# Attention block on one core: the last head's division by 128x8 columns, and the first image through two DMA queues

## The chip, the cores and the metric

The kernel runs on one core of one Trainium2 chip. A core has a matrix engine (TensorE, PE in the profile; its weight loads are listed apart as PEld), a vector engine (DVE), a scalar engine (ACT), GpSimd (POOL) and a sync engine (SP) that here only issues DMAs. The metric is the device time of one execution in microseconds; the time of a kernel is the median of several runs.

## What is computed

The block is a group norm, multi-head self-attention over the 1024 pixels of each image, a projection and a residual, all in float32. There are 16 images of 512 channels, 4 heads of 128 channels and 8 groups. Cut to what matters:

```python
b, c, h, w = x.shape                      # 16, 512, 32, 32
xn = group_norm(x, 8) * gamma + beta
qkv = einsum('oc,bchw->bohw', qkv_w, xn) + qkv_b
q, k, v = heads(split(qkv, 3))            # 4 heads of 128
attn = softmax(einsum('bhnd,bhmd->bhnm', q, k) * 128 ** -0.5)
out = einsum('bhnm,bhmd->bhnd', attn, v)
out = einsum('oc,bchw->bohw', proj_w, out) + proj_b
return x + out
```

## The kernel before

**Steps.** The fast path runs 16 images x 4 heads x 8 blocks of 128 keys, 512 steps in all. A step makes scores of 128 keys against 1024 queries in two halves of 512 (L607), takes the exponential on ACT without subtracting a maximum (L612), adds it to a running sum `tot` on DVE (L620), and multiplies `v` by it into `po` (L675), which ACT copies to `os_` (L682). The projections (q and k, v, output) are done with Strassen's seven products, two levels deep for most of them; the sums that they need are DVE subtractions and additions, and their pieces are spread over the steps by a written plan (`plan_head`).

**Order.** The program is traced in Python order, and a planner that simulates the engines then orders each engine's instructions: it takes what is ready by its own model of time, earlier-traced work first. Each engine runs its list strictly in that order. Tiles come from pools; tiles with one tag share that tag's buffers, and a tile waits until its buffer is free. The PSUM tag "s" of pool `ps_s` has two buffers. DMAs issued by SP and ACT use eight completion semaphores in turn, so a DMA waits until the one eight before it in the planner's order has landed.

**Division.** After a head's eight steps the softmax denominators are needed: the sum of `tot` over its 128 partitions. For all heads but the last, `denominators` (L622) makes them in a small 32x32 form, takes the reciprocal there, and broadcasts it to 128 partitions through DRAM into `rinv`; `divide` multiplies `os_` by it. The last head of the last image uses `last_division` (L648): a product with a 128x128 matrix of ones puts the denominators of 512 queries on all partitions at once; DVE takes the reciprocal of that 128x512 tile and multiplies `os_` by it, for each half. `last_span` (L660) takes the reciprocal of the reciprocal on 32 partitions to recover `l`, and keeps the sum over the queries of max(l, 1/l) in the last column of `spans`. At the end all of `spans` is summed (`total`, `most`) and compared with a limit; if it is over, the whole block is computed again on a general path.

**The last projection** (`last_projection`, L748) follows the last step with one level of Strassen. `x_` and `y_` are two PSUM banks each (`lx`, `ly`), `z_` (`lz`) takes tag "s". Products 1 and 5 do not read the last head's output; product 2 reads it in its second chunk, and so does product 6, whose operand `t2` is a DVE subtraction (L253, `sums_of_b`). `copy` keeps `x_` on ACT before the next product accumulates into it. `add` (L764) adds a product to the residual tile `y`, and its last call for a tile issues the output DMA.

**The start.** `load_x(0)` issues the first image as eight transfers of 256 KB on SP (L199). DVE takes statistics of each (`bn_stats` L40, `bn_aggr` L41), then a short chain of small operations on PE, DVE and POOL gives scale and shift, and DVE and ACT normalise. Behind the image, SP loads weights of v (`wv`, L373) and of q and k (`st`, L287); ACT loads five small vectors (L215: `gamma_sb` and so on) and its function table (L206).

Of the kernel before, what the change touches and what calls it, by code (L numbers as in the profile page):

```python
# [10 lines left out]
F32 = mybir.dt.float32  # L11
I32 = mybir.dt.int32
AF = mybir.ActivationFunctionType
ALU = mybir.AluOpType
AX = mybir.AxisListType

P = 128
HEADS = 4
GROUPS = 8
EPS = 1e-5  # L20
BLK = 32
HALF = 512
# [65 lines left out]
def attention_block(  # L88
# [35 lines left out]
    with ExitStack() as fast:  # L124
        fast_path(fast, tc, x, sources, out, consts, flag, dims)
# [28 lines left out]
def fast_path(ctx, tc, x, sources, out, consts, flag, dims):  # L154
# [5 lines left out]
    nc = tc.nc  # L160
    B, C, N, NCC, NH2, NB, GC, SCALE = dims
# [6 lines left out]
    one = ctx.enter_context(tc.tile_pool(name="one", bufs=1))  # L168
# [8 lines left out]
    lpool = ctx.enter_context(tc.tile_pool(name="l", bufs=1))  # L177
    upool = ctx.enter_context(tc.tile_pool(name="u", bufs=2))
    ypool = ctx.enter_context(tc.tile_pool(name="y", bufs=4))
    gn = ctx.enter_context(tc.tile_pool(name="gn", bufs=2))  # L180
    dpool = ctx.enter_context(tc.tile_pool(name="rows", bufs=4, space=DRAM))
    kept = ctx.enter_context(tc.tile_pool(name="kept", bufs=1, space=DRAM))
    ps_s = ctx.enter_context(tc.tile_pool(name="ps_s", bufs=2, space=PSUM))
# [1 line left out]
    ps_a = ctx.enter_context(tc.tile_pool(name="ps_a", bufs=2, space=PSUM))  # L185


    spans = one.tile([BLK, B * HEADS], F32, name="spans")
    ones = one.tile([BLK, 1], F32, name="ones")
    ones_sq = one.tile([P, P], F32, name="ones_sq")  # L190
    xs, xb, vs, qs, ks, os_, ob = {}, {}, {}, {}, {}, {}, {}
    mvs, scaled = {}, {}

    def load_x(b):
        for c in range(NCC):
            xs[b, c] = xpool.tile([P, N], F32, tag="x", name=f"x_{b}_{c}")
            for half in range(NH2 if b == 0 else 1):
                i = ts(half, HALF) if b == 0 else ds(0, N)
                nc.sync.dma_start(xs[b, c][:, i], x[b, ts(c, P), i])  # L199


    load_x(0)
# [46 lines left out]
    def sums_of_b(b, rows=(1, 2), chunks=range(KC)):  # L249

        def sub(o, i, j):
            for k in chunks:
                nc.vector.tensor_sub(b[o][k], b[i][k], b[j][k])  # L253

        if 1 in rows:
            sub("t1", "b12", "b11")
        if 2 in rows:
            sub("t2", "b22", "t1")
            sub("t3", "t2", "b11")
            sub("t4", "b21", "t2")  # L260
# [336 lines left out]
    ps, tot, po, rinv, last_eviction = {}, {}, {}, {}, {}  # L597
    steps = B * HEADS * NB

    def where(s):  # L600
        bh, j = divmod(s, NB)
        return (*divmod(bh, HEADS), j)
# [44 lines left out]

    def last_division(b, h):  # L648

        t = tot.pop((b, h))  # L650
        for half in range(NH2):
            l = ps_s.tile([P, HALF], F32, tag="s", name=f"l_{half}")
            nc.tensor.matmul(l, ones_sq, t[:, ts(half, HALF)], start=True, stop=True)
            i = ts(half, HALF)
            r = lpool.tile([P, N], F32, tag="rinv", name=f"rinv_{b}_{h}") if half == 0 else r
            nc.vector.reciprocal(r[:, i], l)
            nc.vector.tensor_mul(os_[b, h][:, i], os_[b, h][:, i], r[:, i])
        return r

    def last_span(r):  # L660

        l = lpool.tile([P, N // BLK, BLK], F32, tag="tt", name="l_last")
        l = l.rearrange("p c m -> p (c m)")[:BLK, :]
        nc.vector.reciprocal(l, r[:BLK, :])
        nc.vector.scalar_tensor_tensor(
            l, l, 1.0, r[:BLK, :], ALU.mult, ALU.max,
            accum_out=spans[:, B * HEADS - 1 : B * HEADS],
        )

    def weighted_sum(s, half):  # L670
        b, h, j = where(s)
# [47 lines left out]
    late = {}  # L719

    def last_loads(what):


        if what == "x":
            late["y"] = []
            for c in range(NCC):
                t = xpool.tile([P, N], F32, tag="x", name=f"y_{c}")
                nc.sync.dma_start(t, x[B - 1, ts(c, P), :])
                late["y"].append(t)
            return  # L730
        late["w"] = []
        for g in range(4):
            t = qkpool.tile([P, N], F32, tag=f"qk{g % 2}", name=f"wl_{g}")
            t = t.rearrange("p (i m) -> p i m", m=HALF)
            first = 2 * g
            n = slice(1, 2) if g == 0 else slice(0, 2)
            nc.sync.dma_start(t[:, n], store["last"][:, first + n.start : first + 2])
            late["w"] += [t[:, 0], t[:, 1]]
# [9 lines left out]
    def last_projection(b):  # L748


        y, bl = late["y"], ob[b]
        x_, y_, z_, kept_ = {}, {}, {}, {}

        def mm(acc, r, p, first):
            for k in range(KC):
                nc.tensor.matmul(  # L756
                    acc, late["w"][p][:, ds((r * KC + k) * P, P)], bl[FACTORS[p][1]][k],
                    start=(first and k == 0), stop=(k == KC - 1), skip_group_check=True,
                )

        def add(row, r, half, a, done):
            o = 2 * row + r
            t = y[o][:, ts(half, HALF)]
            nc.vector.tensor_add(t, t, a)  # L764
            if done:
                (nc.sync, nc.scalar)[r].dma_start(out[b, ts(o, P), ts(half, HALF)], t)

        def copy(r, n):
            t = upool.tile([P, HALF], F32, tag=n, bufs=1 if n == "u3" else 2, name=f"l_{n}_{r}")
            nc.scalar.copy(t, x_[r])  # L770
            kept_[n, r] = t

        for r in range(2):
            x_[r] = ps_a.tile([P, HALF], F32, tag="x", name=f"lx_{r}")
            mm(x_[r], r, 1, True)
            copy(r, "p1")
        recip = last_division(b, HEADS - 1)
        sums_of_b(bl, (2,), (1,))
        for r in range(2):
            y_[r] = ps_a.tile([P, HALF], F32, tag="y", name=f"ly_{r}")  # L780
            mm(y_[r], r, 5, True)
            add(0, r, 0, kept_["p1", r], False)
        for r in range(2):
            z_[r] = ps_s.tile([P, HALF], F32, tag="s", name=f"lz_{r}")
            mm(z_[r], r, 2, True)
            add(0, r, 0, z_[r], True)
        for r in range(2):
            mm(x_[r], r, 6, False)
            copy(r, "u2")
        last_span(recip)  # L790
        for r in range(2):
            add(0, r, 1, kept_["u2", r], False)

        total = gn.tile([BLK, 1], F32, tag="total", name="total")
        nc.vector.tensor_reduce(total, spans, AX.X, ALU.add)
        for r in range(2):
            mm(x_[r], r, 7, False)
            copy(r, "u3")
            add(1, r, 1, kept_["u3", r], False)
            add(1, r, 1, y_[r], True)  # L800
        most = ps_s.tile([P, HALF], F32, tag="s", name="most")
        nc.tensor.matmul(most[:1, :1], total, ones, start=True, stop=True)
        ok = gn.tile([1, 1], F32, tag="fine", name="fine")
        nc.vector.tensor_scalar(ok, most[:1, :1], LIMIT, None, ALU.is_le)
        fine.append(ok)
        for r in range(2):
            mm(x_[r], r, 4, False)
            add(1, r, 0, x_[r], True)
        for r in range(2):
            mm(y_[r], r, 3, False)  # L810
            add(0, r, 1, y_[r], True)

    def plan_head(b, h):
# [7 lines left out]
        elif h == 1:  # L821
# [6 lines left out]
            if b + 1 == B:  # L828
                plan[0].append(lambda: last_loads("x"))
            else:  # L830
                plan[0].append(lambda: load_x(b + 1))
                spread(plan, [lambda c=c: stats_chunk(b + 1, c) for c in range(NCC)], 2, 6)
                plan[5].append(lambda: stats_group(b + 1))
                plan[6] += [
                    lambda c=c, half=half: normalise(b + 1, c, half)
                    for half in range(NH2) for c in range(NCC)
                ]
        elif b + 1 == B:
            if h == 2:
                plan[0].append(lambda: last_loads("w"))  # L840
                plan[2].append(last_bias)
            else:
                os_[b, h] = opool.tile([P, N], F32, tag="o", name=f"o_{b}_{h}")
                plan[3].append(lambda: o_blocks(b))
                plan[3].append(lambda: sums_of_b(ob[b], (1,)))
                plan[4].append(lambda: sums_of_b(ob[b], (2,), (0,)))
        elif b + 1 < B:
            if h == 2:
                plan[0].append(lambda: x_sums(b + 1))
                spread(plan, staggered([v_units(b + 1, jj) for jj in range(2)]), 1, NB)  # L850
            else:
                spread(plan, staggered(qk_groups(b + 1, 0)), 0, NB)
# [34 lines left out]
    for s in range(steps + 1):  # L887
        units = []
        if s < steps:
            b, h, j = where(s)  # L890
# [5 lines left out]
        for half in range(NH2):  # L896
# [6 lines left out]
            n = (len(units) + 1) // 2  # L903
            run(units[half * n : (half + 1) * n])
        if s > 0:
            del ps[s - 1]

    last_projection(B - 1)
    nc.vector.tensor_scalar(flag, fine[0], -1.0, 1.0, ALU.mult, ALU.add)

# [130 lines left out]
```

## Time and profile before

| what | value |
|---|---|
| median of 4 runs | 3237.96 us (3236.84 to 3238.95) |
| the profiled execution | 3237.0 us, span 3235.1 us, granted clock 0.999 |
| DVE busy 3200 to 3205, 3205 to 3210, 3210 to 3215.4 | 4.98, 5.00, 5.40 us |
| `rinv<-l` 128x512 reciprocal (L656) | 2 x 3320 ns |
| `l_last<-rinv` 32x1024 reciprocal (L664) | 1 x 6532 ns |
| `l_last` 32x1024 max and sum (L665) | 1 x 1206 ns |
| `l<-tot,ones_sq` (L653) | 4 PE instructions, 592 ns each |
| `o<-o,rinv` 128x512 (L657) | 2 x 650 ns |
| x transfers (L199) | 8 x 256 KB, 4.0 us median from issue to landing |
| DMA traffic | 357.32 MB, mean 110 GB/s over the span |

A time on a row of the profile is the instruction's own duration; matmuls are pipelined, so their starts, not their ends, give the pace. One f32 matmul of the program shows as two PE instructions. "Idle before, releaser" is how long an engine stood still and what ended the wait. The span is the time between the first and last instruction of the profiled execution; the rest of its 3237.0 us lies around it.

### The profile page before, as it was taken

To read this page: it belongs to the slowest core of one execution; us is meant where nothing else is said; L and a number is where in the kernel's file an instruction comes from. 1 tells how busy PE (TensorE), PEld (TensorE's weight loads), DVE (VectorE), ACT (ScalarE), POOL (GpSimd) and SP (SyncE) were. 2 spreads that over 40 slices of the span, in tenths; PEclk is the share of its full clock that TensorE was granted. 3 is DMA by queue.
4 is the path that set the end of the run, shared out by engine and by line. 5 is a ranking of instruction groups with operands and counts; after the bars stand their busy time and mean duration, and the time that the engine had idled before them with its cause. 6 is when DMAs were issued, how large, how long until landed. Compare 5 with 4: busy or idle time off the path is not lost.

```text
span 3235.1 us, 31036 instructions
## 1 busy us (share of the span) xinstructions
PE 3203.2 (99%) x10666; PEld 2005.9 (62%) x10666; DVE 2464.4 (76%) x4392; ACT 1246.6 (39%) x2168; POOL 16.3 (1%) x20
## 2 busy tenths in 40 slices
PE   7999999999999999999999999999999999999998
PEld 6566666666666666666666666666666666666653
DVE  7858689586886868868687785877859678596785
ACT  2433334333343343433334333343434334333442
POOL 0000000000000000000000000000000000000000
PEclk9999999999999999999999999999999999999999
DMA  5423333233232333333333332333323333233330
GB/s 175 150 80 126 113 104 128 80 118 123 91 133 82 123 111 108 117 98 118 112 107 109 108 118 97 114 115 110 115 92 115 108 113 124 79 126 109 108 128 34
DMA packets 114837, 357.32 MB, mean 110 GB/s; under 512 B 15472, under 2 KB 27248, under 8 KB 114672
## 3 DMA queue, kind: packets, MB, share of 16 engines
q1 hardware_dynamic: 113376, 354.20, 32.6%
q8 instruction: 86, 1.41, 0.2%
q10 hardware_dynamic: 1296, 1.06, 0.1%
q14 instruction: 79, 0.65, 0.1%
HBM read 308.10 MB, written 47.12 MB: 110 GB/s over the span
## 4 chain that ended last, share of the span: by engine, by line
PE 92%; DVE 6%; ACT 1%; issue 1%; POOL 0%; DMA 0%; SPq 0%; DVEq 0%; POOLq 0%; ACTq 0%
PE s L607 25%; PE po L675 25%; PE qk_x L469 12%; PE qk_y L469 9%; PE v_x L548 7%; PE v_y L548 5%; PE pp_x L469 5%; PE pp_y L469 4%; DVE tot L620 2%; DVE y L588 1%; DVE y L591 1%; DVE pp_r L501 1%; POOL rstd L64 0%; PE lx L756 0%; DVE pp_r L484 0%
## 5 line engine op out<-in xcount | busy, mean ns | idle before, releaser
L607 PE MATMUL s<-qk,qk 128*128 128x512 f32 x2048 | 1049.0, 594 | 1.8 <-DVE qk L519 1.3
L675 PE MATMUL po<-p,v 128*128 128x512 f32 x2048 | 1045.4, 593 | 0.7 <-ACT p L612 0.7
L612 ACT ACTIVATE p<-s 128x512 f32<-128x512 f32 x1024 | 611.1, 597 | 1065.7 <-PE s L607 1028.4
L620 DVE TENSOR_TENSOR tot<-tot,p 128x1024 f32<-128x1024 f32 x385 | 468.9, 1218 | 312.8 <-ACT p L612 309.4
L675 PEld LDWEIGHTS po<-p,v 128*128 128x128 f32 x2048 | 387.1, 190 | 442.6 <-issue 416.6
L607 PEld LDWEIGHTS s<-qk,qk 128*128 128x128 f32 x2048 | 386.3, 190 | 112.3 <-issue 54.8
L469 PEld LDWEIGHTS qk_x<-qk_t,w 128*128 128x128 f32 x1344 | 250.5, 190 | 200.5 <-issue 139.9
L469 PE MATMUL qk_x<-qk_t,w 128*128 128x256 f32 x1344 | 358.1, 383 | 1.7 <-ACT qk_u L397 1.5
L397 ACT COPY qk_u<-qk_x 128x512 f32<-128x512 f32 (+1 forms) x256 | 136.4, 533 | 238.4 <-PE qk_x L469 237.3
L484 DVE TENSOR_TENSOR qk_r<-qk_y,qk_u 128x512 f32<-128x512 f32 (+1 forms) x256 | 158.3, 618 | 23.6 <-PE qk_y L469 21.6
L548 PE MATMUL v_y<-w_v,x 128*128 128x256 f32 x720 | 173.0, 380 | 0.0
L548 PEld LDWEIGHTS v_x<-w_v,xt 128*128 128x128 f32 x720 | 136.8, 190 | 57.0 <-issue 43.0
L548 PE MATMUL v_x<-w_v,xt 128*128 128x256 f32 x720 | 170.1, 379 | 0.0
L548 PEld LDWEIGHTS v_y<-w_v,x 128*128 128x128 f32 x720 | 135.6, 190 | 55.0 <-issue 40.9
L469 PE MATMUL pp_x<-pp_t,w_proj 128*128 128x256 f32 x630 | 167.8, 383 | 0.0
L469 PEld LDWEIGHTS pp_x<-pp_t,w_proj 128*128 128x128 f32 x630 | 117.2, 190 | 73.7 <-issue 44.5
L469 PE MATMUL qk_y<-x,w 128*128 128x256 f32 x512 | 141.8, 379 | 0.0
L519 DVE SCALAR_TENSOR_TENSOR qk<-qk_r,qkb_sb,qk_r 128x512 f32<-128x512 f32 x192 | 135.3, 745 | 1.5 <-ACT qk_r L482 0.4
L568 DVE TENSOR_TENSOR v<-v_y,v_u 128x512 f32<-128x512 f32 x64 | 43.6, 682 | 113.2 <-ACT v_u L397 68.8
L397 ACT COPY pp_u<-pp_x 128x512 f32<-128x512 f32 (+1 forms) x120 | 63.9, 532 | 160.8 <-PE pp_x L469 150.0
L484 DVE TENSOR_TENSOR qk_r<-qk_y,qk_p 128x512 f32<-128x512 f32 (+1 forms) x128 | 79.1, 618 | 56.3 <-PE qk_y L469 56.3
L469 PEld LDWEIGHTS qk_y<-x,w 128*128 128x128 f32 x512 | 97.3, 190 | 39.7 <-issue 21.0
(167 smaller groups left out, 3449.8 us busy)
## 6 DMA issues: line engine op xcount, KB each, us to landing
w<-kept SPq DMA_DIRECT2D x90, 896.0 KB, 4.6
w_v<-kept_v SPq DMA_DIRECT2D x60, 768.0 KB, 4.4
w_proj<-kept_proj SPq DMA_DIRECT2D x45, 896.0 KB, 4.9
rinv<-row SPq DMA_DIRECT2D x63, 512.0 KB, 3.7
out_y<-y SPq DMA_DIRECT2D x124, 256.0 KB, 2.2
x<-in_x SPq DMA_DIRECT2D x60, 512.0 KB, 4.2
y<-in_x SPq DMA_DIRECT2D x120, 256.0 KB, 3.9
w<-kept SPq DMA_DIRECT2D x30, 448.0 KB, 3.4
```

The lines of the kernel that those rows point to most:

```text
L397: nc.scalar.copy(t[n][:, :width], t["x"][:, :width])
L469: nc.tensor.matmul(acc[:, ts(i, Q)], have["w"][:, i, SLOTS[an], :], inner(i, bn), start=(first and i == 0), stop=True, skip_group_check=True,)
L484: nc.vector.tensor_add(dst, view(a), view(c))
L501: nc.vector.tensor_add(part(2, 0), part(1, 1), part(2, 0))
L519: nc.vector.scalar_tensor_tensor(st[b, h][:, ts(half, HALF)], a[:, r, :], qkb_sb[:, i : i + 1], c[:, r, :], ALU.add, ALU.add,)
L548: nc.tensor.matmul(acc[:, ts(g, HC)], xb[b][bn][k][:, ts(2 * jj + g, P)], wi[:, k, :], start=(first and g == 0 and k == 0), stop=(k == KC ...
L568: nc.vector.tensor_add(dst, view(a), view(c))
L588: nc.vector.scalar_tensor_tensor(t, a[:, r, :], projb_sb[:, o : o + 1], t, ALU.add, ALU.add)
L607: nc.tensor.matmul(sc, ks[b, h][:, ts(j, P)], qs[b, h][:, ts(half, HALF)], start=True, stop=True)
L612: nc.scalar.activation(ps[s][:, ts(half, HALF)], sc, AF.Exp, scale=SCALE)
L620: nc.vector.tensor_add(tot[b, h][:, i], tot[b, h][:, i], ps[s][:, i])
L675: nc.tensor.matmul(po[b, h][:, i], vs[b, h // 2][:, h % 2, j, :], ps[s][:, i], start=(j == 0), stop=(j == NB - 1),)
```

## The change

`load_x` issues the second half of each channel tile of the first image on ACT's queue instead of SP's.

`last_division` no longer puts the sums on all partitions. Eight products use a 128x128 block of `tot` as the stationary operand and one column of ones as the moving one, so that the denominators of 1024 queries stand in a PSUM tile as 128x8. DVE takes the reciprocal of that; ACT copies `l` itself. DVE then builds `r_blocks`, 128 x 8 x 128, as the identity times each column of the reciprocal (two products of 128x512, both inputs broadcast), and a product of ones with each half puts the reciprocals on all partitions in PSUM (`rows`), from where DVE multiplies `os_`. The identity is made on POOL (a memset and a select) in the last image's third head, in a buffer of tag "y".

`last_span` becomes an element-wise maximum of the two 128x8 tiles and a sum along the free axis into `span`, traced later than before. `spans` has one column less, and `most` adds up two products, one of `total` and one of `span`.

```diff
-    spans = one.tile([BLK, B * HEADS], F32, name="spans")
+    spans = one.tile([BLK, B * HEADS - 1], F32, name="spans")
...
-                nc.sync.dma_start(xs[b, c][:, i], x[b, ts(c, P), i])
+                eng = nc.scalar if b == 0 and half == 1 else nc.sync
+                eng.dma_start(xs[b, c][:, i], x[b, ts(c, P), i])
...
         t = tot.pop((b, h))
+        acc = ps_s.tile([P, HALF], F32, tag="s", name="l_last")
+        for j in range(NB):
+            nc.tensor.matmul(
+                acc[:, j : j + 1], t[:, ts(j, P)], ones_sq[:, 0:1], start=(j == 0), stop=True,
+                skip_group_check=True,
+            )
+        r = lpool.tile([P, NB], F32, tag="part", name="r_last")
+        nc.vector.reciprocal(r, acc[:, :NB])
+        l = lpool.tile([P, NB], F32, tag="l", name="l_col")
+        nc.scalar.copy(l, acc[:, :NB])
+        blocks = lpool.tile([P, NB, P], F32, tag="tt", name="r_blocks")
+        n = NB // NH2
         for half in range(NH2):
-            l = ps_s.tile([P, HALF], F32, tag="s", name=f"l_{half}")
-            nc.tensor.matmul(l, ones_sq, t[:, ts(half, HALF)], start=True, stop=True)
+            i = ts(half, n)
+            nc.vector.tensor_mul(
+                blocks[:, i, :], late["ident"].unsqueeze(1).to_broadcast([P, n, P]),
+                r[:, i].unsqueeze(2).to_broadcast([P, n, P]),
+            )
+        for half in range(NH2):
+            rows = ps_s.tile([P, HALF], F32, tag="s", name=f"rows_{half}")
+            nc.tensor.matmul(
+                rows, ones_sq, blocks[:, ts(half, n), :].rearrange("p j q -> p (j q)"),
+                start=True, stop=True,
+            )
             i = ts(half, HALF)
-            r = lpool.tile([P, N], F32, tag="rinv", name=f"rinv_{b}_{h}") if half == 0 else r
-            nc.vector.reciprocal(r[:, i], l)
-            nc.vector.tensor_mul(os_[b, h][:, i], os_[b, h][:, i], r[:, i])
-        return r
+            nc.vector.tensor_mul(os_[b, h][:, i], os_[b, h][:, i], rows)
+        return l, r
...
-    def last_span(r):
-        l = lpool.tile([P, N // BLK, BLK], F32, tag="tt", name="l_last")
-        l = l.rearrange("p c m -> p (c m)")[:BLK, :]
-        nc.vector.reciprocal(l, r[:BLK, :])
-        nc.vector.scalar_tensor_tensor(
-            l, l, 1.0, r[:BLK, :], ALU.mult, ALU.max,
-            accum_out=spans[:, B * HEADS - 1 : B * HEADS],
-        )
+    def last_span(l, r):
+        worst = lpool.tile([P, NB], F32, tag="worst", name="worst_last")
+        span = gn.tile([P, 1], F32, tag="span", name="span_last")
+        nc.vector.tensor_max(worst, l, r)
+        nc.vector.tensor_reduce(span, worst, AX.X, ALU.add)
+        return span
...
+        late["ident"] = ypool.tile([P, HALF], F32, tag="y", name="ident")[:, :P]
+        make_identity(nc, late["ident"])
...
-        last_span(recip)
         for r in range(2):
             add(0, r, 1, kept_["u2", r], False)
+        span = last_span(l, recip)
...
-        nc.tensor.matmul(most[:1, :1], total, ones, start=True, stop=True)
+        nc.tensor.matmul(most[:1, :1], total, ones, start=True, stop=False)
+        nc.tensor.matmul(most[:1, :1], span, ones_sq[:, 0:1], start=False, stop=True)
```

## The prediction

> **What bounds the kernel now.** I read the page's first part first, then the chain of waits over the last 50 us, then stage windows at both ends, where the change lies, and last the DMA issues of the start.
>
> ```profile
> PE 3203.2 (99%) x10666; PEld 2005.9 (62%) x10666; DVE 2464.4 (76%) x4392; ACT 1246.6 (39%) x2168; POOL 16.3 (1%) x20
> ```
>
> TensorE (PE) sets the time: 99% busy. A change off its path is worth something only where PE stands idle. PE has two such places that this change touches: the lead-in before its dense work (its first matmul is at 11.85 us) and the last projection. The chain of waits there (start, us, what):
>
> ```profile
> 3200.71 6.48 DVE rinv L656 x2
> 3207.19 1.14 DVE o L657 x2
> 3208.33 6.45 DVE l_last L664
> 3214.78 0.56 DVE ot L253
> 3215.34 0.04 issue
> 3215.38 7.11 PE lx L756 x12
> ```
>
> For 14.6 us the chain runs through VectorE (DVE): two reciprocals of 128x512, two products, and the 6.45 us reciprocal of `last_span`, which DVE took ahead of the subtraction (L253) that PE needed. The stage windows (PE, PEld, DVE, ACT, POOL busy, then granted clock) show PE's side:
>
> ```profile
> 3199.20:3209.60 10.40, 10.25 (x25) 4.28 (x23) 9.58 (x6) 0.59 (x1) 0.00 (x0) 1.00 0.00 0
> 3209.60:3215.38 5.78, 0.49 (x2) 0.00 (x0) 5.78 (x3) 0.00 (x0) 0.00 (x0) 0.99 0.00 0
> 3215.38:3218.79 3.41, 3.41 (x4) 1.17 (x4) 3.41 (x5) 0.59 (x1) 0.00 (x0) 0.52 0.25 94
> 3218.79:3229.71 10.92, 10.88 (x27) 4.48 (x26) 6.51 (x14) 1.76 (x3) 0.00 (x0) 1.00 0.33 122
> ```
>
> PE nearly stops from 3209.8 to 3215.38, and comes back at a granted clock of 0.52 for four instructions. So the stall costs twice.
>
> **The tail, step by step.** An f32 product of 128x512 is two PE instructions. Eight `ly` instructions run from 3200.92 to 3204.35: 0.429 us each. From the first `l` instruction (3199.20) to the last addition (3229.71), which the end follows, are 30.51 us. In it are 52 such instructions (4 `l`, 16 `ly`, 8 `lz`, 24 `lx`): 52 x 0.429 = 22.3, with `most` 22.4. Lost: 8.1 us. Of these 5.56 are the stall (3209.82 to 3215.38), 1.69 the slow clock (3.41 - 4 x 0.429), 0.32 a wait for `rinv` before 3207.25, and some 0.5 is small change.
>
> Removed on PE: the 4 `l` instructions. Added: 4 for `rows` (same size, so 1.72 against 1.72), 2 for `most` (some 0.1), and the small products: 8 of them, 16 instructions with a full 128x128 weight load and one column. The trace has this shape in `bias_of_v`:
>
> ```profile
> 127.15 0.95 PE L698 MATMUL pb<-vb_sb,st_a 128*128 128x1 f32 x8
> 127.96 1.11 PE L607 MATMUL s<-qk,qk 128*128 128x512 f32 x2
> ```
>
> Eight start within 0.81 us, 0.101 each; so 16 cost 1.62. New PE work: 48 x 0.429 + 1.72 + 1.62 + 0.2 = 24.1 us. With no wait left the tail would win 30.5 - 24.1 = 6.4; I leave the 0.5 of small change standing: **-5.9**.
>
> Do the new waits stay covered? Small products end at 3199.20 + 1.62 = 3200.8. Then DVE: 0.17 handover (as `pb` to L702), the reciprocal of 128x8 at about 0.2 (bounds: 0.16, a 128x4 operation, and 0.335, the 32x32 reciprocal of L637; its 8 elements a lane are nearest the first), the first `r_blocks` product 0.69. That product has both inputs broadcast, which no row shows; bounds are 0.54 (L84, 128x512 with one tensor input) and 1.22 (twice the elements, L620), and I take L253's 0.69. `rows_0` 0.86 with 0.2 of handover, product with `os_` 0.69: 3203.6. `rows_1` follows `rows_0`, so the second half is done near 3204.5, or 3205.4 if `rows_0` sits behind an `ly` product (0.86), and the `t2` subtraction near 3206.1. Meanwhile PE has `ly` (3.43), the first-chunk `lx` of product 6 (1.72) and `rows` (1.72): work until 3207.7. So about 1.6 us to spare; block products at 1.22 (+1.06) still fit. Without that cover each lost us is paid in full.
>
> The new waits: the PSUM tag "s" has two buffers, so `lz_0` now waits until DVE has read `rows_0`, and `lz_1` until it has read `rows_1`. All of PE's queue stands behind such a wait. Products 7, 4 and 3 wait for their usual copies. The ACT copy of `l` lies between 0.20 (primer) and 0.59 (L770), and ACT was idle 18.2 us there; `last_span` shrinks to two small operations of about 0.2 (L795), in a DVE that loses 14.4 us of work and gains 1.8. The identity on POOL (a memset, one select, waiting for a `y` buffer) is bounded by nothing and a few us of POOL, which is 1% busy; heads 2 and 3 of the last batch lie between it and its use, each 8 x 3.43 us. Zero.
>
> The page TensorE: Matmul & The Clock Gate, section Part 1, says that an idle window of about 3.4 us halves the clock; the 0.52 after 5.6 idle us agrees. By it a new wait up to 3 us would cost only itself.
>
> **The head.** Statistics of the first image are one DVE pass over eight transfers. When each starts:
>
> ```profile
> 5.19 0.69 DVE L40 BATCH_NORM_STATS2 st<-x 128x6 f32<-128x512 f32 x1 [0.75 <-DMA x<-in_x]
> 7.73 0.69 DVE L40 BATCH_NORM_STATS2 st<-x 128x6 f32<-128x512 f32 x1 [0.17 <-DMA x<-in_x]
> 9.23 0.69 DVE L40 BATCH_NORM_STATS2 st<-x 128x6 f32<-128x512 f32 x1 [0.81 <-DMA x<-in_x]
> 11.38 0.21 DVE L41 BATCH_NORM_AGGREGATE mv<-st 128x2 f32<-128x12 f32 x1
> ```
>
> and why they come late, in the waits of SP's queue up to 11 us, with the stages' DMA share and GB/s last:
>
> ```profile
> SPq L199 <- DMA gamma_sb<-in_gamma: 1.4, 1, 1.4
> SPq L199 <- DMA x<-in_x: 1.2, 2, 0.9
> ```
>
> ```profile
> 3.00:6.00 3.00, 0.00 (x0) 0.00 (x0) 1.47 (x3) 0.00 (x0) 0.00 (x0) 1.00 1.07 347
> 6.00:9.00 3.00, 0.00 (x0) 0.00 (x0) 2.21 (x5) 0.00 (x0) 0.00 (x0) 1.00 0.81 225
> ```
>
> SP and ACT share eight completion semaphores in turn: the fifth image transfer waits for `gamma` to land, later ones for earlier image halves. So SP issues the last half at 6.25, and the rate falls from 347 to 225 GB/s. After the change each queue issues four halves in turn, about 0.46 us apart: all out by 2.6, taking all eight semaphores, with the five small loads behind them. By 3.0 us 0.19 MB had moved (62 GB/s); the other 1.91 MB at 347 GB/s end at 8.5, so the last pair lands near 8.7 against 10.63 now. Its two passes and aggregation (0.69 + 0.60 + 0.24) end at 10.2 instead of 11.59: **-1.4**. Bounds: -2.0 (DVE never waits after 3.75) and +1.1 (three weight loads of 128 KB, 0.38 each at 347 GB/s, get in between and nothing else is won). DVE and then PE run through to the first head with no slack, so the shift is kept.
>
> What is late next: `wv_a` now waits for image halves to land. By the same turn-taking its eighth issue comes near 11.0 instead of 10.65 and lands near 14.4; L877 needs it at 17.41 - 1.4 = 16.0. Covered by 1.6 us. `gamma` and its fellows, queued on ACT behind the halves, land by about 12; L66 needs `gamma` at 13.6. ACT's table load (1.28 us) ran beside its DMA issues before.
>
> One rule speaks against this edit. The page DMA: Bandwidth & Descriptors, section Issuing engines are not separate DMA queues, says that a second queue uses the same 16 engines and saves issue time alone, usually a small thing. Read strictly, it makes the head worth nothing and the sum 3232.1. The rows above stand against it: waits before an issue are what left 225 of 347 GB/s.
>
> **Sum.** -1.4 - 5.9 = -7.3. The profiled execution took 3237.0 (span 3235.1): 3229.7. It stands 1.0 below the median 3237.96 of the runs, so the median to expect is **3230.7**.
>
> **Rivals.** (1) The head's gain is lost: weights or the small loads arrive later than DVE wants them, or the engines share out as before. For: every SP load shifts onto semaphores of the image. Against: 1.6 us of slack. 3237.96 - 5.9 = 3232.1. (2) The planner puts `rows` straight behind the small products; PE then waits for reciprocal and block product (1.1), and `lz_0` for its buffer (1.4). For: it put `l_last` ahead of L253 before. Against: `ly` is ready earlier. Tail -3.4: 3233.2. (3) Slower: the planner's order of the fifteen steady batches shifts with the new start. Starts of PE instructions beyond their pitch now add up to 1.45 us a batch (0.3 and 1.15 in alternate stretches of 100 us). If a batch loses twice that, 15 x 1.45 = 21.8 more: 3252.5. It decides for slower from 0.92 a batch, (7.3 + 6.5) / 15. Against: later DMAs are all on SP and unchanged in number. (4) The change does not shorten the chain because DVE again takes something long first: its longest operation left is 0.69, so hardly possible.
>
> **How the numbers follow.** Forecast 0.62 (own range 3229 to 3232.3), rival 1 0.14, rival 2 0.14, rival 3 0.06, more gain than summed (-9) 0.04. Within 0.2% (6.5 us, about what a measurement tells from no change) lie rivals 1 and 2 and a tenth of the forecast's chance: the limit is 3231.5. So faster 0.60, same 0.34, slower 0.06. The range 3228.4 to 3234.8 leaves out rival 3 and the tips.
>
> **What would show it.** Right: no PE gap over 0.5 us between 3192 and the end, clock 1.00 there, `rows` to last addition some 6 us shorter; the last L41 near 10.2; first `v_x` near 15.0. Wrong: PE waiting on `r_blocks` or on DVE's product before `lz`; a wait of L877 for `wv_a`; batches in the middle longer than before.

## The result, and the profile after

The changed kernel takes **3231.82 us** (median of 31 runs, 3230.08 to 3233.88) against 3238.17 us for the kernel before (51 runs, 3236.43 to 3240.86): a ratio of 0.998, 95% interval 0.9975 to 0.9985. That is 6.35 us less, where 7.3 had been forecast. The profiled executions stand at 3237.0 and 3230.76 us, their spans at 3235.13 and 3228.99. Three points that both traces have cut the difference of 6.14 into parts (us):

| point | before | after | difference |
|---|---|---|---|
| first v product starts | 16.65 | 16.92 | +0.27 |
| first product of q and k | 38.52 | 37.74 | -0.78 |
| first product of the last projection (`lx`) | 3194.83 | 3194.18 | -0.65 |
| last addition | 3229.71 | 3223.30 | -6.41 |
| span | 3235.13 | 3228.99 | -6.14 |

So the tail, from the first `lx` to the last addition, went from 34.88 to 29.12 us: -5.76. The head gave 0.65, though its statistics end 1.20 earlier, and the last output took 0.27 longer to leave. The steady middle, from the first scores to the first `lx`, is 3128.43 and 3128.56 us.

**The tail.** The first part of the page has DVE with 12 us less work and PE with as much as before:

```profile
PE 3202.6 (99%) x10684; PEld 2007.6 (62%) x10684; DVE 2452.8 (76%) x4392; ACT 1246.7 (39%) x2169; POOL 17.6 (1%) x22
```

The chain of waits over the last projection (start, us, what) now stays on PE, where before it ran 14.6 us through DVE:

```profile
3198.72 1.68 PE l_last L656 x16
3200.40 1.82 PE ly L777 x4
3202.23 1.72 PE rows L674 x4
3203.94 1.72 PE ly L777 x4
3205.66 3.43 PE lz L777 x8
3209.09 6.87 PE lx L777 x16
```

Each piece begins where the one above it ended; the stage windows show the same (PE, PEld, DVE, ACT and POOL busy, granted clock, DMA share, GB/s): 24.76 us of PE in 24.80, at full clock.

```profile
3198.50:3207.00 8.50, 8.50 (x33) 4.83 (x32) 5.70 (x11) 0.75 (x2) 0.00 (x0) 1.00 0.00 0
3207.00:3215.00 8.00, 8.00 (x20) 3.48 (x19) 2.86 (x5) 1.76 (x3) 0.00 (x0) 1.00 0.17 66
3215.00:3223.30 8.30, 8.26 (x23) 3.25 (x21) 4.93 (x10) 0.59 (x1) 0.00 (x0) 1.00 0.37 137
```

DVE's side of the first 8 us, in its timeline (start, us, instruction, and in brackets its idle time before and what ended it):

```profile
3200.44 0.21 DVE L661 RECIPROCAL r_last<-l_last 128x8 f32<-128x8 f32 x1 [2.08 <-PE l_last L656]
3200.75 1.30 DVE L668 TENSOR_TENSOR r_blocks<-ident,r_last 128x512 f32<-128x512 f32 x2
...
3203.12 0.69 DVE L679 TENSOR_TENSOR o<-o,rows 128x512 f32<-128x512 f32 x1 [0.21 <-PE rows L674]
3203.98 0.69 DVE L679 TENSOR_TENSOR o<-o,rows 128x512 f32<-128x512 f32 x1 [0.17 <-PE rows L674]
3204.70 0.69 DVE L255 TENSOR_TENSOR ot<-o,o 128x512 f32<-128x512 f32 x1
```

The reader is to see two things. The reciprocal fell from 3.32 us twice to 0.21 once: a lane now has 8 elements in one instruction instead of 512 in each of two. And `t2`, the last line, ends at 3205.39, before PE has done its second four `ly` instructions: nothing waits for DVE.

**The head.** The same two windows as before show that the image now arrives without a pause (347 and 225 GB/s then):

```profile
3.00:6.00 3.00, 0.00 (x0) 0.00 (x0) 1.32 (x3) 1.13 (x2) 0.00 (x0) 1.00 1.04 373
6.00:9.00 3.00, 0.00 (x0) 0.00 (x0) 2.84 (x7) 0.00 (x0) 0.00 (x0) 1.00 1.07 372
```

Its last half lands at 8.91 us instead of 10.63. DVE's timeline tells what became of that:

```profile
10.18 0.21 DVE L41 BATCH_NORM_AGGREGATE mv<-st 128x2 f32<-128x12 f32 x1
...
12.50 0.16 DVE L62 TENSOR_SCALAR ve<-pv 128x4 f32<-128x4 f32 x1 [0.68 <-PE pv L60]
13.64 0.69 DVE L899 TENSOR_TENSOR wv_s<-wv_a,wv_a 128x512 f32<-128x512 f32 x1 [0.98 <-DMA wv_a<-in_qkv_wT]
14.25 0.15 DVE L66 TENSOR_TENSOR sc<-rstd,gamma_sb 128x4 f32<-128x4 f32 x1
...
15.72 0.68 DVE L382 TENSOR_TENSOR wv_s<-wv_a,wv_s 128x512 f32<-128x512 f32 x1
16.32 1.00 DVE L84 TENSOR_SCALAR x<-x,sc,sh 128x512 f32<-128x512 f32 x2
```

The aggregation ends at 10.39 instead of 11.59, as was to be. But then come four additions of v's weights (L899, L380, L381, L382; in the kernel before the same four, L877 and L378 to L380, ran behind the normalising, from 17.41 on). The planner now has them between the variance and the normalising: DVE waits 0.98 us for a weight to land and works 2.7 us on them, between the small operations that lead to scale and shift. DVE begins the first normalised tile, which the first v product waits for, at 16.32 instead of 15.58. What the head gained nevertheless, it gained later: in the kernel before, PE's products came unevenly between 20.47 and 22.7 us, their starts 0.9 us late in all against the usual 0.215 us. Part of it is this wait for DVE, which the changed kernel does not have:

```profile
21.16 0.70 PE L548 MATMUL v_y<-wv_s,x 128*128 128x256 f32 x2 [0.31 <-DVE x L253]
```

### The profile page after: what moved, and what is told of

The parts are those of the page before. It is cut to its first block, busy times and chain, and to the rows that moved or that the text cites. A ratio compares the mean times of both kernels' runs of the same rounds, so it can differ in the third digit from the quotient of the medians.

```text
span 3229.0 us, 31083 instructions
## 1 busy us (share of the span) xinstructions
PE 3202.6 (99%) x10684; PEld 2007.6 (62%) x10684; DVE 2452.8 (76%) x4392; ACT 1246.7 (39%) x2169; POOL 17.6 (1%) x22
## 4 chain that ended last, share of the span: by engine, by line
PE 92%; DVE 5%; ACT 1%; DMA 1%; POOL 0%; issue 0%; ACTq 0%; DVEq 0%; POOLq 0%
PE po L694 25%; PE s L609 25%; PE qk_x L471 12%; PE qk_y L471 9%; PE v_x L550 7%; PE v_y L550 5%; PE pp_x L471 4%; PE pp_y L471 4%; DVE tot L622 2%; DVE y L590 1%; DVE y L593 1%; DVE pp_r L503 1%; POOL rstd L64 0%; PE lx L777 0%; DVE pp_r L486 0%
```

## The experiments

The medians are of 11 runs each, beside the kernel before on the same chip (3238.14 to 3238.58 there). "Tail" is the time from the first `lx` to the last addition in the profiled execution: 34.88 before, 29.12 after.

| run | what | median us | ratio, 95% | tail us | first v | first q, k |
|---|---|---|---|---|---|---|
| head only | before + two queues | 3238.21 | 0.9998 (0.9989 to 1.0007) | 34.88 | 16.59 | 37.41 |
| tail only | after, one queue | 3231.75 | 0.9979 (0.9970 to 0.9988) | 29.12 | 16.38 | 38.58 |
| sums held | after, weight sums behind the normalising | 3231.25 | 0.9977 (0.9968 to 0.9986) | 29.11 | 15.87 | 38.00 |
| sums on POOL | after, weight sums on POOL | 3234.25 | 0.9987 (0.9978 to 0.9996) | 29.11 | 18.35 | 42.04 |
| span late | before, `last_span` behind the sums | 3237.45 | 0.9997 (0.9988 to 1.0006) | 34.28 | 16.79 | 38.66 |
| l kept | before, `l` copied instead of inverted back | 3231.09 | 0.9979 (0.9970 to 0.9988) | 28.26 | 16.90 | 39.22 |
| kept, two queues | l kept + span late + two queues | 3230.76 | 0.9977 (0.9968 to 0.9986) | 27.96 | 16.61 | 37.44 |
| small twice | after, small products twice | 3235.77 | 0.9992 (0.9983 to 1.0001) | 30.90 | 17.01 | 40.05 |
| blocks twice | after, block products twice | 3232.79 | 0.9982 (0.9973 to 0.9991) | 29.11 | 17.32 | 40.28 |
| warm ten | after, 10 warm-up products | 3231.83 | 0.998 (0.9971 to 0.9989) | 29.11 | 17.27 | 38.42 |
| kept, warm ten | kept, two queues + 10 warm-up products | 3230.61 | 0.9977 (0.9968 to 0.9986) | 27.96 | 17.16 | 38.74 |
| warm from start | kept, two queues + sums held + early warm-up | 3229.97 | 0.9975 (0.9966 to 0.9984) | 27.96 | 16.68 | 37.48 |

**Each half of the change alone.** The kernel before with only the two queues, and the changed kernel with all eight image transfers back on SP:

```diff
-                nc.sync.dma_start(xs[b, c][:, i], x[b, ts(c, P), i])
+                eng = nc.scalar if b == 0 and half == 1 else nc.sync
+                eng.dma_start(xs[b, c][:, i], x[b, ts(c, P), i])
```

> The kernel before with the first image loaded through two queues, the last head's division as it was. The profile of the changed kernel shows the middle of the program 0.65 to 0.8 us earlier than before and the stretch from the first l product to the last addition 5.8 us shorter. Theory: the two edits do not touch each other, so this kernel gains 0.65 us (span near 3234.4), against 1.4 forecast; its tail keeps the 5.6 us stall. Rival: the head gains the forecast 1.4 and something in the new tail takes it back, then the span is near 3233.7.

> The changed kernel with the whole first image on SP's queue. Theory: all that is left is the tail, 5.8 us less than before (span near 3229.5), with no stop of PE over 0.5 us in it. Rival: part of the gain of the changed kernel lies in the middle of the program or in the way the head changes the planner's order, then this kernel gains less than 5 us and the first one more than 0.65.

The tail alone gives 6.8 us of median, as much as the whole change; the head alone 0.4, less than two medians of 11 runs can tell apart (its own runs lie between 3236.45 and 3240.08). In the profiles the head alone puts the first `lx` 0.64 us earlier than before, as in the changed kernel (0.65), and the two tails repeat to 0.01 us. So the two edits hardly touch each other.

**Who took the head's gain.** One kernel holds v's weight sums behind the last normalising operation on DVE (`norm.last`, the instruction behind which they are issued, is set there), the other moves them to POOL, behind its one operation in the chain of the statistics:

```diff
-    before_power = norm.last
     warm(7, "warm")
     for half in range(NH2):
         for c in range(NCC):
             normalise(0, c, half)
+    before_power = norm.last
```

```diff
-        nc.vector.tensor_add(wv["s1"], wv["a21"], wv["a22"])
+        nc.gpsimd.tensor_add(wv["s1"], wv["a21"], wv["a22"])
...
+        self.last = nc.gpsimd.tensor_tensor(rstd, ve, self.neghalf, ALU.pow)
```

> The changed kernel with DVE's four weight sums for v held behind its normalisation, where the kernel before had them. Theory A: the missing 0.75 us of the head went into these sums, which the planner put ahead of scale and shift, so that v's first product starts at 16.92 instead of 16.65; held back, the first product starts near 15.3 and all later work 0.7 us earlier. Theory B: DVE's total of sums is the limit up to the sixth product, whose operand needs four image sums and two weight sums; then the first product starts near 15.3 too, but PE stops later for DVE and the middle gains nothing or loses up to 0.5 us.

> The changed kernel with the four weight sums for v made on POOL instead of DVE, behind POOL's rstd. Theory A and theory B both say that scale and shift come near 14.35 and the first product of v near 15.3. Under B, 2.4 us of DVE work are gone as well, so PE runs nearly without a stop from there: all later work 1.0 to 1.6 us earlier than in the changed kernel. Rival: POOL's sums of 128x512 take several us each or slow DVE down beside them, so that the sixth product waits and the gain is under 0.5 us or negative.

Held back, the sums free the start: the first normalised tile is begun at 14.82 instead of 16.32, and the first v product comes at 15.87 (15.3 had been expected), right behind the last warm-up product. So it was their place in DVE's list that kept v late in the changed kernel. But the first q and k product is no earlier for it (38.00 against 37.74), and the median moves by 0.6 us. In this profile seven of the first v products start 0.43 us apart instead of 0.215:

```profile
15.87 3.22 PE L550 MATMUL v_x<-wv_a,x 128*128 128x256 f32 x8
```

The six gaps between them lose 1.3 us, more than the 1.05 that v starts earlier. This half pace has a part of its own below. On POOL the sums are worse than in either place. DVE's timeline there, and POOL's:

```profile
14.23 1.23 DVE L66 TENSOR_TENSOR sc<-rstd,gamma_sb 128x4 f32<-128x4 f32 x1 [1.15 <-POOL rstd L64]
15.49 0.16 DVE L73 TENSOR_TENSOR t<-mu,sc 128x4 f32<-128x4 f32 x1
15.69 1.12 DVE L75 TENSOR_TENSOR sh<-beta_sb,t 128x4 f32<-128x4 f32 x1
16.84 2.86 DVE L84 TENSOR_SCALAR x<-x,sc,sh 128x512 f32<-128x512 f32 x2
```

```profile
14.17 1.27 POOL L899 TENSOR_TENSOR wv_s<-wv_a,wv_a 128x512 f32<-128x512 f32 x1
15.52 1.27 POOL L380 TENSOR_TENSOR wv_s<-wv_s,wv_a 128x512 f32<-128x512 f32 x1
```

In this run a DVE operation of four elements a lane that runs beside a POOL addition takes 1.23 us instead of 0.15, and two normalising operations take 2.86 instead of 1.00. The two small ones end with the POOL addition that runs beside them (15.46 and 15.44; 16.81 and 16.79).

**Is it the new division, or only the reciprocal that is gone?** Three versions of the kernel before. The first moves `last_span`, with its 6.45 us reciprocal, behind the subtractions. The second takes that reciprocal away: ACT copies the 32 rows of `l` that it needs from PSUM, and the two reciprocals of 128x512 stay. The third has both and the two queues.

```diff
-                nc.vector.tensor_sub(b[o][k], b[i][k], b[j][k])
+                b["last"] = nc.vector.tensor_sub(b[o][k], b[i][k], b[j][k])
...
-        last_span(recip)
+        with tc.issue_after(bl["last"].ins):
+            last_span(recip)
```

```diff
             nc.tensor.matmul(l, ones_sq, t[:, ts(half, HALF)], start=True, stop=True)
+            nc.scalar.copy(lk[:, i], l[:BLK, :])
...
-        nc.vector.reciprocal(l, r[:BLK, :])
```

> The kernel before with one thing changed: last_span's two DVE operations are issued behind the last of the subtractions that PE waits for. Theory: the stall of 5.56 us and the slow clock after it (1.69) come from the order, the 6.45 us reciprocal taken ahead of L253, and not from the two reciprocals of the division. Then PE does not stop after lz and its clock stays at 1.00; but DVE still has 7.7 us of span work, so the additions come late and the end is set by DVE: a gain of 3.5 to 5 us. Rival: the division's two reciprocals (6.5 us) are the bound; then the stall stays, moved, and the gain is under 2 us.

> The kernel before, but l is kept by two copies of 32x512 on ACT straight from PSUM, so that the second reciprocal of 32x1024 is gone; the division itself is as before, with two reciprocals of 128x512 and no small products. Theory: the whole gain of the tail lies in the removed second reciprocal; this kernel gains 6.5 to 7.2 us in the tail, more than the changed kernel's 5.8, since PE is spared the 1.7 us of small products and DVE's two long reciprocals lie beside PE work. Rival: the reciprocals of the division still hold PE up by some us, and the gain is under 5.

> The last kernel with the span's operation behind the last subtraction, and the first image through two queues. Theory: 0.65 from the head and 7.0 to 7.3 from the tail: 7.7 to 8.0 us less than before, some 1.4 less than the changed kernel. Rival: the waits between ACT's copy and DVE's reading of the same PSUM tile cost what the small products cost, and it is within 0.5 us of the changed kernel.

Moving it gains 0.6 us in the tail where 3.5 to 5 had been expected. The chain of waits of that run shows where the rest went:

```profile
3211.64 0.60 DVE y L764
3212.24 6.45 DVE l_last L664
3218.69 0.55 DVE y L764
3219.24 1.14 DVE l_last L665 x2
```

and PE's timeline what stood behind it:

```profile
3221.16 0.18 PE L803 MATMUL most<-ones,total 32*1 32x1 f32 x2 [3.64 <-DVE total L796]
3222.44 1.92 PE L756 MATMUL lx<-ot,wl 128*128 128x512 f32 x2 [1.09 <-ACT l_u L770]
```

The stall only changed its name. PE runs its list in order, and `most`, which needs `total`, stands ahead of the next `lx`. Here too the clock falls behind the stall, to 0.50 from 3222.63 to 3226.04. Nor was the expected rival right, by which the two reciprocals of the division would hold PE up: without the `last_span` reciprocal, and with those two kept, the tail is 28.26 and 27.96 us, shorter than in the changed kernel. The chain of the run with two queues:

```profile
3198.88 0.87 PE l L654 x2
3199.75 0.02 issue
3199.78 0.58 ACT l_last L659
3200.36 0.02 issue
3200.38 6.58 DVE rinv L661 x2
3206.96 0.04 issue
3207.01 2.84 PE lz L757 x6
```

The two old reciprocals are still on the chain, but PE has `ly` and other ready products to do under them: in that run it is busy 23.09 of 23.50 us from 3198.8 to the last addition. So one removed operation gives the whole gain; the small products, the blocks and `rows` replace reciprocals that PE's other work covers, and cost PE 16 small instructions, 1.70 us. The version with both parts and two queues has a median 1.1 us below the changed kernel's, with runs (3229.29 to 3232.31) that overlap with its runs.

**What the new parts cost.** The small products written twice (the second set into PSUM columns that nothing reads), and each block product written twice:

```diff
+        for j in range(NB):
+            nc.tensor.matmul(
+                acc[:, NB + j : NB + j + 1], t[:, ts(j, P)], ones_sq[:, 0:1], start=False,
+                stop=True, skip_group_check=True,
+            )
```

```diff
-        for half in range(NH2):
+        for half in (0, 0, 1, 1):
             i = ts(half, n)
             nc.vector.tensor_mul(
```

> The changed kernel with the eight small products made twice, the second set into columns that nobody reads. Theory: PE is the bound all through the tail, so 16 more instructions cost their pace of 0.101 to 0.107 us, 1.6 to 1.75 us, and the end moves by as much. Rival: another engine sets the end there, and the end moves by less than 0.8 us.

> After with each of the two products that make the diagonal blocks written twice (VectorE, 2 x 0.65 us more; the second writes the same values), so that the products of ones with the blocks come later. Theory A (the forecast's: the way from l to its spread inverse has 1.6 us to spare under the last projection's first products): the tail from the first x product of the last projection to the last addition stays at 29.1 us within 0.2, the median at after's 3231.8 within 0.4. Theory B (there is no such spare time; TensorE stands still for the blocks, or the multiplications come too late for the second y group): up to 1.3 us more, tail 30.4, median 3233.1.

PE work is paid in full: 16 more small instructions, tail +1.78. DVE work under cover costs the tail nothing: the four block products take 2.50 us instead of 1.30, and the tail stays at 29.11. PE's timeline shows how: the planner puts six `ly` instructions ahead of `rows` instead of four, and the rest behind.

```profile
3202.54 2.82 PE L777 MATMUL ly<-o,wl 128*128 128x512 f32 x6
3205.20 1.88 PE L674 MATMUL rows<-r_blocks,ones_sq 128*128 128x512 f32 x4
```

Both medians are higher than their tails make them: 3235.77 where 1.78 more would make 3233.6, and 3232.79 where nothing more would make 3231.8. In both profiles most of the rest lies in the first v products, in a head that no edit touched; the first q and k product, behind them, comes 2.3 and 2.5 us later than in the changed kernel. Eight of the first v products in the timeline of the small-twice run, and in that of the changed kernel:

```profile
17.01 3.78 PE L550 MATMUL v_x<-wv_a,x 128*128 128x256 f32 x8 [1.38 <-DVE x L84]
```

```profile
16.92 1.99 PE L550 MATMUL v_x<-wv_a,x 128*128 128x256 f32 x8 [1.26 <-DVE x L84]
```

The same eight instructions at half the pace: their starts are 0.43 us apart instead of 0.215, up to 21.4 us.

**The half pace at the start.** I took PE's idle time ahead of v (1.26 us in the changed kernel, none before) for its cause, and filled it:

```diff
-    warm(7, "warm")
+    warm(10, "warm")
```

> After with ten warm-up products instead of seven; nothing else differs. In the profile of after the last warm-up product begins at 15.24 and ends about 15.45 to 15.66, and the first v product comes at 16.92: TensorE has nothing for 1.3 us. Three products more (six records 0.213 us apart, 1.28 us) fill that gap to about 16.7 and so should not delay the first v product. Theory A (the idle 1.3 us makes it likelier that the first v products run at the half pace, 0.43 instead of 0.21 us apart, as ten pairs did in the small-twice run): the dear runs go, the median falls by 0.5 to 1.5 us against after's 3231.8, to 3230.3 to 3231.3, and the runs lie closer together than after's 3.8 us. Theory B (the moment at which the clock goes up has nothing to do with the gap): median and spread as after, 3231.8 within 0.4. Theory C (the further products are in v's way): up to 1.3 us slower, 3233.

> The two-queue kernel that keeps the division of before (the span's part alone cut and put behind the last sums; median 3230.8), with ten warm-up products instead of seven. Theory A (the gap ahead of the first v product, 15.64 to 16.61 in its profile, lets the half pace in): 3229.3 to 3230.3, and nearer together than 3229.3 to 3232.3. Theory B: 3230.8 within 0.4. Theory C (1.28 us of products against a gap of 1.0): up to 0.5 us slower.

That theory fell: both medians are within 0.2 us of those without the three products. The runs lie somewhat closer together (2.7 and 2.1 us instead of 3.8 and 3.0), but 11 runs against 31, and 11 against 11, show little by that. The last kernel keeps PE at work from 1.4 us on, and holds the weight sums back:

```diff
+    warm(26, "early")
     for c in range(NCC):
         stats_chunk(0, c)
     stats_group(0)
-    before_power = norm.last
-    warm(7, "warm")
+    warm(14, "warm")
```

> The two-queue kernel that keeps the division of before (median 3230.8), with two edits at the start: the sums of v's weights held behind the last normalise, as in the sums-held run, and TensorE kept at work from 1.4 us on, by 26 warm-up products ahead of the statistics' products and 14 instead of 7 behind them. Theory A (the pace goes up only once TensorE has worked without a stop for some time, 3.3 to 6.5 us in the profiles so far; work from 1.4 us on settles that before v): the 14 products run at twice the pace, 0.107 us a record, and end near 15.3, the first v product comes near 15.9, and no v product is at the half pace. Against the 3230.8, -0.7 for the earlier v and about -0.6, half of the 1.3 us that six slow pairs cost in the sums-held run: 3229.5 (3229.0 to 3230.2), with the runs nearer together than 3.0 us. Theory B (the gaps between the small statistics' products, 10.9 to 12.3, put the pace back; the 14 run at 0.213 a record): they end near 18.3, v is 1.7 us later than in the kept kernel, and the median is 3231.5 to 3232.5.

The median, 3229.97, is in theory A's range and the lowest of all, but A is not borne out by it: the runs lie 4.0 us apart, not under 3.0, and overlap with those of "kept, two queues", and in the profile the first v product comes at 16.68, not 15.9, behind warm-up products that ran slow again. Windows cut where the pace of PE's instructions changes:

```profile
1.40:6.30 4.90, 4.82 (x22) 4.82 (x23) 1.48 (x4) 1.49 (x2) 0.00 (x0) 1.00 0.90 298
6.30:9.70 3.40, 3.40 (x32) 3.39 (x30) 3.40 (x9) 0.00 (x0) 0.00 (x0) 1.00 0.99 338
9.70:13.10 3.40, 2.07 (x17) 1.80 (x16) 1.42 (x8) 0.00 (x0) 0.84 (x1) 1.00 0.74 193
13.10:16.50 3.40, 3.40 (x19) 3.40 (x18) 3.09 (x9) 2.60 (x4) 0.17 (x1) 0.52 0.88 252
16.50:20.00 3.50, 3.50 (x18) 3.11 (x18) 3.50 (x7) 0.92 (x2) 0.00 (x0) 0.98 0.98 362
...
57.60:61.00 3.40, 1.78 (x6) 0.59 (x4) 3.40 (x5) 1.17 (x2) 0.00 (x0) 1.00 0.00 0
61.00:64.40 3.40, 3.15 (x8) 2.52 (x9) 2.37 (x7) 0.19 (x1) 0.00 (x0) 0.50 0.00 0
```

The products of 128x128 start 0.213 us apart until 6.4 us, 0.11 apart after it, and 0.213 apart again from 13.2 to 16.6. So the pace went up, fell after a stretch in which PE was busy 2.07 of 3.40 us with idle gaps of 0.69 and 0.64 us ahead of the two products of the statistics, and went up once more. It fell again at 61.0, after another stretch with waits, and came back at 64.4. That cost time too: from the first q and k product to the first scores it is 28.83 us here and 28.17 in the kernel "kept, two queues", so the first scores are no earlier for all that was done at the start (66.31 against 65.61). The warm-ten profile has such a fall at 62.3; the changed kernel's has none there. The trace's own record of the granted clock puts the five changes at 6.39, 13.22, 16.63, 61.00 and 64.42 us: 2, 1, 13 and 1 times 3.413 us apart. In the kernel before, those at 16.95 and 3215.24 are 937 times that apart.

The granted clock says 0.52 in the fourth window, but 1.00 in the first, where the pace is the same: until its first change that column is not to be relied on, and the distance of the starts is.

## Why the prediction was right, and where it was off

**The tail was sized rightly.** From the first `l` product to the last addition the forecast made 24.6 us (30.51 - 5.9); it is 24.74. Term by term: small products 1.62 forecast, 1.70 measured; reciprocal 0.2 and 0.21; block product 0.69 and 0.65; from the first small product to the second multiplication's end 5.3 forecast, or 6.2 with `rows` behind an `ly` product, and 6.1 with it there; to the end of `t2` 6.9 and 6.8. The 1.6 us to spare are borne out as far as they were tried: 1.2 us more of block products moved nothing. No wait came for the "s" buffers, the second `most` product cost some 0.1 us as forecast, and the identity nothing that can be seen. What the forecast did not ask is which of the removed operations the stall hung on. It listed all three reciprocals as the chain; the runs that keep the two of the division show that taking away the 6.45 us one of `last_span` is enough.

**The step that failed** is in the head: "DVE and then PE run through to the first head with no slack, so the shift is kept." The shift itself was nearly right (-1.20 at the last aggregation, -1.4 forecast). It was not kept: the first v product, forecast "near 15.0", came at 16.92, and 0.65 us are left at the first `lx`. I had moved the operations behind the statistics as one block, in the order of before. They are a planner's order, and data that comes earlier changes it. The forecast asked when L877 would need its weight ("Covered by 1.6 us"), and the weights were in time for that: the last lands at 13.45, before the 14.4 forecast. But the sums were put 3.8 us earlier in DVE's list, ahead of the normalising, and there one waited 0.98 us. Holding them back brought the first v product to 15.87, which shows the cause of the late start; that the gain did not come through even then is the work of the half pace, six gaps of 0.21 us extra in that profile.

**The rivals.** The measured 3231.82 lies nearer to rival 1 (head's gain lost, 3232.1) than to the forecast (3230.7). Its reason, weights that arrive later than DVE wants them, is half of what happened: they came earlier than forecast, and DVE wanted them earlier still. By the profiles the gain is not lost but halved; by the medians of the head alone (-0.4) and of the tail alone it cannot be told from nothing. Rival 2 fell: `rows` stands behind four `ly` instructions. Rival 3 fell: the steady middle differs by 0.13 us in 3128. Rival 4 fell too, but the run with `last_span` behind the sums shows what it looks like: 6.45 us at another place, for a gain of 0.6.

**The two rules.** The page DMA: Bandwidth & Descriptors of the Trainium skill, section Issuing engines are not separate DMA queues, would have given the head nothing, or little, as a second issuing engine saves issue time alone. Here the last half of the image landed 1.7 us earlier, with SP's waits ahead of the image's issues gone. Whether that took a second queue is not shown: the edit also put the five small loads behind the image, and no run has all eight halves on SP ahead of them. Of the kernel's time the rule came close, for a reason that it does not speak of.

The second rule did not hold here as I used it. From the page TensorE: Matmul & The Clock Gate, section Part 1, I took that "a new wait up to 3 us would cost only itself". In the run with warm-up from the start a stretch with 1.3 us of idle time in it brought the pace down, which then stayed at half for 3.4 us. The same section says that the window is about 3.4 us long and free-running, not started by the kernel; the changes at 6.4, 13.2, 16.6, 61.0 and 64.4 us agree with that. Its table asks for an idle window before the clock goes down, and here windows that were busy for 2.07 and 1.78 us of 3.40 were enough. How much work keeps the clock up is open: in the kernel before, PE was busy for 1.67 us only from 3208.42 to 3211.83, and the clock stayed at 1.00 for the next 3.4 us. So busy time alone does not decide it.

## What to carry to other kernels

When a transfer is made earlier under a planner, ask which work becomes ready with it and where the planner will put that; a shift is not handed on along an order that it changes itself. When the end of a kernel stalls on one long operation, first try to take that operation away alone: here a copy by an idle engine in place of the reciprocal of a reciprocal gave the whole gain of the tail and 0.9 to 1.2 us more than the rebuilt division, while moving the operation gave 0.6. Work is worth removing from an engine that something waits for, and free to add under cover: in this tail 1.2 us more on DVE cost nothing, 1.7 us more on PE cost 1.78.

## What was not expected of the hardware

- **The pace of the first v products differs between versions whose start is the same program.** With the start of before, 0 gaps between v instructions were 0.43 us in the profiled execution of before, 1 in span late, 6 in tail only, 7 in l kept; with the changed start, 0 in the changed kernel, in head only and in "kept, two queues", 9 in small twice and in blocks twice. Each costs 0.21 us, so an execution can lose about 2 us there, against the 3 to 4 us between the runs of one kernel. The two profiles compared at the top happen to have none. Why nearly all runs of the small-twice kernel lie as if they had it, and whether the fixed windows alone make the rest, stays open.
- **POOL beside DVE.** Additions of 128x512 on POOL, 1.27 us each, stretched small DVE operations from 0.15 to 1.23 and 1.12 us; both ended within 0.02 us of a POOL addition.
